# A graph network's hops on one core: twelve load slots for the weight columns in the room of the residual features, and gathered rows split in tiles of four

## The chip, the cores and the metric

The kernel runs on one core of a Trainium2 chip. The metric is the device time of one execution in microseconds, as the median of several runs; less is better. All inputs start in the core's DRAM and the output ends there.

## The reference, cut to what matters

The program is a stack of four residual graph blocks over 6250 nodes with 128 features each, and 106,250 directed edges (17 edges end in each node on average). Every block is followed by a layer norm over `x + block(x)`. The first three blocks are usual graph convolutions. The last one, which takes most of the time, has three layers, and each layer sends its features three times over the weighted edges. These nine sendings are the *hops*:

```
w = dinv[src] * edge_attr * dinv[dst]
h = node
for l in range(NUM_LAYERS):                       # 3
    out = h @ W[l, 0]
    x = h
    for k in range(1, K + 1):                     # K = 3
        x = jax.ops.segment_sum(w[:, None] * x[src], dst, num_segments=N)
        out = out + x @ W[l, k]
    y = h + out + bias[l]
    h = relu(layernorm(y) * gamma[l] + beta[l])
...
x = _layernorm(x + h)          # the x that came into this block: the residual
```

The weights of the edges are the same in all nine hops. The residual `x` is made before the first hop and read only after the last.

## The kernel before, in words

**Windows and chunks.** The nodes lie in 49 windows of 128. Destination windows are put together into 13 chunks of four windows, some of three, so that one chunk has up to 512 destination columns. A chunk fills one bank of PSUM (128 features x 512 nodes).

**A hop has two parts.** The first nine chunks (33 windows; six chunks are 512 columns wide, three are 384) are *dense*. Their edge weights have been scattered into a full matrix in DRAM, `weights`. For one chunk, TensorE multiplies the features of source window 0, 1, ... 48 (`tables[h]`) with the 128 x 512 block of that matrix which belongs to the window and the chunk, and sums all 49 products in one bank, `acc` (L1086). The matrix is too large for SBUF, so it is streamed from DRAM in every hop: SP issues one load for every two windows (`STEP = 2`, 512 KB or 384 KB, L453 in `columns`, called at L1084). The loads go round through six slots of the tile `weighed` (`LOADS = 6`, L913). This makes 225 loads and 441 window products in a hop; each window product shows as two instructions in the trace, hence 7938 of them.

The other 16 windows are *gathered*. Each has 19 gathers (`KG`); one gather fetches 128 rows of 128 features by index from the hop's table in DRAM (`stored`), 304 in a hop. POOL issues them one after another (L1018) into a ring of 32 row slots, `rows` (`SLOTS`). ACT then scales a fetched tile by the edges' weights into the left half of a tile `both`, rounded to TensorE's format (L1050); VectorE puts what the rounding lost into the right half (L1051). TensorE adds up both halves at once by multiplying them with a matrix of ones and zeros, `oh`, that says which row goes to which node (L1054). VectorE makes `oh` for five gathers at a time (L1034). There are 14 tiles `both` (L1049), one for each gather under way.

**What sets the order.** TensorE's order is written out by hand. The class `Stream` is a planner: it keeps a clock of its own, adds planned costs to it (a window product 0.86 us, a gathered product 0.12, a gather on POOL 1.26, a landing 7.0), and puts a gathered product between the window products at the time at which it plans its row to have landed. The block at the end runs under `tc.manual_schedule`, so that TensorE follows this order strictly: when one instruction waits, all behind it wait. `AHEAD` (L983) is 28, four less than the row slots: so many gathers may be asked for ahead of those taken. The other engines execute their instructions in their own program order as well, and wait on semaphores that the engines post to each other. SP's queue holds almost only the column loads in this stage; a load waits until TensorE has finished with the slot that it overwrites. ACT's scaling waits for the row to have landed and for TensorE to have finished with the `both` that it overwrites.

**The ends of chunks.** When a chunk's sum is ready, `hop_end` multiplies it with small matrices, updates `hid` (the layer's sum), and stores the next hop's features in DRAM (`store`, L891, from ACT's queue). The next hop's first gather needs all windows of the hop to have been stored, so each hop has a stretch at its start without gathers. In the last hop (`h == 8`) VectorE adds the residual, `xr` (L963), a last norm follows, and ACT's queue stores the result.

**The residual.** `xr` is a table in SBUF of 49 x 128 numbers for each of 128 partitions. The stage before the hops (L895 to L906, "g2") makes it chunk by chunk: `norm(xr[:, ws], r)` writes it (L899), and the first hop's features and `hid` are worked out from it. It then stays in SBUF through all nine hops.

Of the kernel before, what the change touches and what calls it, by code (L numbers as in the profile page):

```python
# [33 lines left out]
F32 = mybir.dt.float32  # L34
# [13 lines left out]
P = 128  # L48
N = 6250
E = 106250  # L50
D = 128
# [30 lines left out]
RPP = -(-(ROWS + P + KX * P // KD + 1) // P)  # L82
L = RPP * KD

SLOTS, LOADS, STEP, HOTS = 32, 6, 2, 5
GROUPS = -(-KG // HOTS)
F_KEY, F_DST = 0, KD + 2 * J
F_CELL, F_LOW, F_W = F_DST + KD, F_DST + 2 * KD, F_DST + 3 * KD
# [272 lines left out]
def usual_way(ctx, tc, a, out, dram, ident, part, first, recs, edges, counts, weights, fills, empty):  # L361
# [31 lines left out]
    def table(name, room, dt=F32):  # L393
        return tabs.tile([P, NW, D], dt, name=name, tag=f"room{room}")
# [19 lines left out]
    def turned(x, d=D):  # L414

        n = x.shape[1]
        pt = bank()
        for j in range(n):
            nc.tensor.transpose(pt[:d, j * P:(j + 1) * P], x[:, j, :], ident[:])  # L419
        t = work.tile([P, CW], F32, name="xT", tag="xT")  # L420
        nc.scalar.copy(t[:d, :n * P], pt[:d, :n * P])
        return t[:d]

    def times(n, xt, w, d=D):
        pm = bank()
        for j in range(n):
            nc.tensor.matmul(pm[:, j * d:(j + 1) * d], xt[:, j * P:(j + 1) * P], w, start=True, stop=True)  # L427
        return pm[:, :n * d].rearrange("p (n d) -> p n d", d=d)
# [398 lines left out]
    with tc.tile_pool(name="counted2", bufs=2) as counted:  # L827
        t2 = table("t2", 0, FR)
        slots = columns_room("room1")
        for c in range(NC):  # L830
            n, ws = of(c)
            nc.scalar.dma_start(xr[:, ws], bases[c][:])
            half = fetched_sums(early_parts[c] if c < AHEAD else halves[c])
            acc = counted_sum(counted, c, both(t1hi, t1lo), turns, slots=slots,
                              since=KNOWN if c < AHEAD else START[c])
            y = mean_conv(c, acc, wt["w2l"][:], half)
            nc.vector.tensor_add(y[:], y[:], xr[:, ws])
            norm(xr[:, ws], y)
            pm = times(n, turned(xr[:, ws]), wt["wconv"][:], DH)
            u = new("u", n, DH)  # L840
            nc.vector.tensor_tensor(u[:], pm, per_node(dinv, ws, DH), op=ALU.mult)
            split(t2[:, ws, :DH], t2[:, ws, DH:], u[:])


        def sym_conv(c, sums, bias, d=D):
            n, ws = of(c)
            r = new("y", n, d)
            nc.vector.tensor_tensor(r[:], sums, per_node(dinv, ws, d), op=ALU.mult)
            nc.vector.tensor_add(r[:], r[:], per_feature(bias, n))
            return r  # L850


        def next_parts(c, hi, lo, x):
            n, ws = of(c)
            u = new("u", n)
            nc.vector.tensor_tensor(u[:], x, per_node(dinv, ws, D), op=ALU.mult)
            split(hi[:, ws], lo[:, ws], u[:])

        def summed(c, parts, w):
            return times(SHAPE[c], evicted(counted_sum(counted, c, parts, turns, own=True), width(c)), w)  # L860

        t3 = table("t30", 2, FR), table("t31", 3, FR)
        for c in range(NC):
            n, ws = of(c)
            agg = evicted(counted_sum(counted, c, lambda s: [t2[:, s, :]], turns, own=True,
                                      slots=slots), width(c))
            pr = bank()
            for j in range(n):
                nc.tensor.matmul(pr[:, j * DH:(j + 1) * DH], agg[:, j * P:(j + 1) * P], stacked[:],
                                 start=True, stop=True)  # L870
            r = sym_conv(c, pr[:, :n * DH].rearrange("p (n d) -> p n d", d=DH), wt["bconv"], DH)
            nc.vector.tensor_scalar_max(r[:], r[:], 0.0)
            po = times(n, turned(r, DH), wt["wlin"][:])
            y = new("h", n)
            nc.vector.tensor_tensor(y[:], po, per_feature(wt["blin"], n), op=ALU.add)
            nc.vector.tensor_add(y[:], y[:], xr[:, ws])
            norm(xr[:, ws], y)
            next_parts(c, *t3, xr[:, ws])

        t4 = table("t40", 0, FR), table("t41", 1, FR)  # L880
        for c in range(NC):
            n, ws = of(c)
            r = sym_conv(c, summed(c, both(*t3), wt["g1"][:]), wt["gb1"])
            nc.vector.tensor_scalar_max(r[:], r[:], 0.0)
            next_parts(c, *t4, r[:])


        hop_out, hid = table("hop", 2), table("hid", 3)
        stored = [dram.tile([P * NW, D], F32, name=f"stored{i}") for i in range(2)]

        def store(ws, i, t):  # L891
            nc.scalar.dma_start(stored[i].rearrange("(p w) d -> p w d", p=P)[:, ws, :], t[:, ws])

        paced.rest()
        for c in range(NC):  # L895
            n, ws = of(c)
            r = sym_conv(c, summed(c, both(*t4), wt["g2"][:]), wt["gb2"])
            nc.vector.tensor_add(r[:], r[:], xr[:, ws])
            norm(xr[:, ws], r)  # L899
            po = times(n, turned(xr[:, ws]), wt["wk"][:, 0])  # L900
            nc.vector.tensor_tensor(hid[:, ws], xr[:, ws], per_feature(wt["bias0"], n), op=ALU.add)
            nc.vector.tensor_add(hid[:, ws], hid[:, ws], po)
            last = nc.vector.tensor_tensor(hop_out[:, ws], xr[:, ws], per_node(dinvw, ws, D), op=ALU.mult)
            store(ws, 0, hop_out)
            for i in range(2 * c, min(2 * c + 2, NG)):
                gathered_edges(i, last.ins)  # L906
# [3 lines left out]
    ohs = ctx.enter_context(tc.tile_pool(name="ohs", bufs=3))  # L910
    ps_g = ctx.enter_context(tc.tile_pool(name="ps_g", bufs=2, space=PSUM))
    fetched_rows = ohs.tile([P, SLOTS, D], F32, name="rows", bufs=1)
    weighed = tabs.tile([P, LOADS, STEP * CW], F32, name="weighed", tag="room1")  # L913

    def hop_end(h, ws, acc, t, now, gathered):

# [43 lines left out]
        nc.vector.tensor_tensor(x[:], x[:], per_feature(wt[f"beta{l}"], n), op=ALU.add)  # L960
        nc.vector.tensor_scalar_max(x[:], x[:], 0.0)
        if h == 8:
            nc.vector.tensor_add(x[:], x[:], xr[:, ws])  # L963
            o = new("u", n)
            norm(o, x)
            for j, w in enumerate(range(ws.start, ws.stop)):
                rows = P if w < NW - 1 else LAST
                nc.scalar.dma_start(out[w * P:w * P + rows, :], o[:rows, j, :])
            return
# [11 lines left out]
    class Stream:  # L981
# [56 lines left out]
        def take(self):  # L1038

            i, k = divmod(self.taken, KG)  # L1040
            if k == 0 and i % 2 == 0:
                self.acc = ps_g.tile([P, CW], F32, name="gacc")
            if k % HOTS == 0:
                g = (self.h * NG + i) * GROUPS + k // HOTS
                self.oh = self.oh_next if g else self.hot(0)
                self.oh_next = self.hot(g + 1) if g + 1 < 9 * NG * GROUPS else None
            x = fetched_rows[:, self.slot(self.taken), :]
            w = gwgt[:, i, k:k + 1]
            both = ohs.tile([P, 2 * D], FR, name="both", bufs=14)  # L1049
            nc.scalar.activation(both[:, :D], x, AF.Copy, scale=w)  # L1050
            nc.vector.scalar_tensor_tensor(both[:, D:], x, w, both[:, :D].bitcast(F32),  # L1051
                                           op0=ALU.mult, op1=ALU.subtract)
            j = i % 2
            nc.tensor.matmul(self.acc[:, j * 2 * D:(j + 1) * 2 * D], self.oh[:, k % HOTS, :], both[:],  # L1054
                             start=k == 0, stop=k == KG - 1)
            self.lands.pop(0)
            self.taken += 1
            self.clock += self.GATHERED
            if k == KG - 1 and GW[i] == PAIRS[i // 2].stop - 1:
                self.ends.append(hop_end(self.h, PAIRS[i // 2], self.acc, tables[self.h + 1], self, True))  # L1060
            if self.taken == NG * KG:
                self.h, self.asked, self.taken = self.h + 1, 0, 0
# [15 lines left out]
        def hop(self, h):  # L1078
            for c in range(ND):
                cw, acc, t = width(c), accumulator(), None  # L1080
                for s in range(NW):
                    self.wait(lambda: (h - 1, s) in self.when)
                    if s % STEP == 0:
                        t = columns(weighed[:, self.loads % LOADS, :], c, weights, F32, STEP, s)  # L1084
                        self.loads += 1
                    nc.tensor.matmul(acc[:, :cw], tables[h][:, s, :], t[:, s % STEP * cw:(s % STEP + 1) * cw],  # L1086
                                     start=s == 0, stop=s == NW - 1)
                    self.clock += self.DENSE * cw / CW
                    self.turn()
                self.ends.append(hop_end(h, of(c)[1], acc, tables[h + 1], self, False))  # L1090
# [368 lines left out]
```

## Time and profile before

| | us |
|---|---|
| median of three runs (7903.20 to 7933.64) | 7911.05 |
| the profiled execution, its own time | 7874.4 |
| its span, first to last instruction | 7872.4 |
| PE, TensorE's matmuls, busy | 5765.3 |
| POOL, the gathers' issue, busy | 4229.2 |
| VectorE busy | 3038.9 |
| ACT busy | 2116.4 |

The profile is of a single execution, which was 0.5% shorter than the median of the timed runs. It names each group of instructions by its line in the kernel, its engine and its operands: `acc<-weighed,hop` is the window product that reads `weighed` and `hop` and writes `acc`. A row of a group ends with the time for which the engine stood idle just before such instructions, and with what it waited for most. "DMA weighed<-weights" there is a column load that had not landed; "PE gacc" is a gathered product that had not been done. "SPq" is SP's queue of DMA issues. "issue" stands for time in which an engine waited for nothing that the profile shows, and "remote" or "another core or an unknown queue" for a release that the profile can't place. This program runs on one core.

Over the whole span the granted clock of TensorE is 0.854 of full speed on average; when TensorE is idle, its clock falls. The nine hops take the last 60% of the span, from 3169 us on.

### The profile page before, as it was taken

Reading aid. Unit: us, or ns where it says so; the run is one execution under the profiler, and the core shown is the slowest. Engines: PE = TensorE matmul, PEld = TensorE weight load, DVE = VectorE, ACT = ScalarE, POOL = GpSimd, SP = SyncE. Lnnn points to the kernel's source line nnn. Section 1 sums busy time; section 2 is a strip of 40 time slices with the busy share of each in tenths; the row PEclk is TensorE's granted clock in tenths of the full one; section 3 lists DMA queues with packets and bytes.
Section 4 is the critical chain, followed back from the end, with each engine's and each line's share of the span. In section 5 each row is a group of like instructions: output and inputs, shape, how many; then the busy total and the mean of one; then the engine's idle time right before and its main releaser. Section 6 shows DMA issues by size and latency. Waiting matters only on the chain. (4 is left out here: it accounts for less than half of the span.)

```text
span 7872.4 us, 74936 instructions
## 1 busy us (share of the span) xinstructions
PE 5765.3 (73%) x20184; PEld 3463.3 (44%) x20184; DVE 3038.9 (39%) x8549; ACT 2116.4 (27%) x4437; POOL 4229.2 (54%) x4207
## 2 busy tenths in 40 slices
PE   1354544339667799788787887987878879878788
PEld 0123333117555688345344453453444534434444
DVE  5344423112555356233332542333335423333355
ACT  1122212115344354222221221222212212222122
POOL 5665455640557411564664655646646456466464
PEclk8676666569878899899898998998989989989899
DMA  7453543013343344577676776776767767777776
GB/s 229 125 163 116 166 134 98 13 30 101 103 115 99 88 139 135 203 264 259 229 261 231 260 241 228 276 249 233 268 235 259 240 225 274 246 248 262 240 275 229
DMA packets 715822, 1532.71 MB, mean 195 GB/s; under 512 B 135525, under 2 KB 346873, under 8 KB 715129
## 3 DMA queue, kind: packets, MB, share of 16 engines
q1 hardware_dynamic: 536448, 1292.14, 49.1%
q0 software_dynamic: 134496, 181.90, 7.9%
q10 hardware_dynamic: 44440, 53.77, 2.0%
q8 instruction: 161, 2.64, 0.1%
q14 instruction: 277, 2.26, 0.1%
HBM read 1334.25 MB, written 193.11 MB: 194 GB/s over the span
## 5 line engine op out<-in xcount | busy, mean ns | idle before, releaser
L1086 PE MATMUL acc<-weighed,hop 128*128 128x512 f32 (+1 forms) x7938 | 3687.9, 584 | 561.7 <-DMA weighed<-weights 532.6
L1018 POOL DMA_INDIRECT rows<-stored,gsrc x2736 | 2709.3, 990 | 2055.4 <-DMA weighed<-weights 715.4
L1086 PEld LDWEIGHTS acc<-weighed,hop 128*128 128x128 f32 x7938 | 1364.6, 198 | 1664.5 <-issue 787.9
L1050 ACT ACTIVATE both<-rows,gwgt 128x128 fp32r<-128x128 f32 x2736 | 1008.5, 397 | 3093.1 <-PE gacc L1054 1400.8
L1054 PE MATMUL gacc<-both,oh 128*128 128x256 f32 x2736 | 1777.1, 657 | 13.3 <-issue 11.8
L1051 DVE SCALAR_TENSOR_TENSOR both<-rows,gwgt,both 128x128 fp32r<-128x128 f32 x2736 | 901.6, 349 | 2112.1 <-issue 1189.1
L492 PE MATMUL acc<-wides,t 128*128 128x512 f32 (+1 forms) x3105 | 948.1, 415 | 444.4 <-issue 221.7
L571 POOL DMA_INDIRECT counts<-cval,celli x833 | 857.3, 1029 | 584.4 <-issue 248.5
L571 POOL DMA_INDIRECT weights<-wval,celli x578 | 609.9, 1055 | 603.2 <-PE acc L492 423.6
L492 PEld LDWEIGHTS acc<-wides,t 128*128 128x128 f32 x3105 | 606.5, 204 | 622.7 <-issue 271.8
L1054 PEld LDWEIGHTS gacc<-both,oh 128*128 128x128 f32 x2736 | 543.5, 199 | 630.9 <-issue 496.7
L481 ACT CAST wides<-slots 128x1024 fp32r<-128x1024 uint8 (+3 forms) x687 | 569.4, 863 | 837.8 <-remote 464.8
L492 PE MATMUL acc<-widev,t 128*128 128x512 f32 (+1 forms) x2034 | 589.6, 400 | 100.4 <-DVE widev L481 61.9
L1034 DVE TENSOR_TENSOR oh<-iota,gdst 128x640 fp32r<-128x640 f16 x576 | 454.5, 789 | 510.6 <-PE gacc L1054 310.0
L695 DVE TENSOR_SCALAR oh<-iota,dloc 128x384 bf16<-128x384 f16 x833 | 228.1, 325 | 900.5 <-remote 462.3
L492 PEld LDWEIGHTS acc<-widev,t 128*128 128x128 f32 x2034 | 387.7, 198 | 178.1 <-DVE widev L481 77.3
L696 PE MATMUL pd<-oh,lw 128*4 128x384 bf16 x833 | 216.0, 382 | 272.3 <-issue 141.5
L481 ACT CAST wides<-cols 128x1024 fp32r<-128x1024 uint8 (+1 forms) x364 | 286.2, 797 | 383.3 <-PE acc L492 166.0
L481 DVE CAST widev<-cols 128x1024 fp32r<-128x1024 uint8 (+1 forms) x364 | 242.9, 671 | 299.3 <-PE acc L492 190.7
L696 PEld LDWEIGHTS <-lw 128*4 128x4 bf16 x833 | 68.7, 91 | 364.3 <-issue 323.3
L481 DVE CAST widev<-slots 128x1024 fp32r<-128x1024 uint8 (+2 forms) x237 | 154.7, 667 | 116.1 <-PE acc L492 37.9
L492 PE MATMUL half<-wides,t 128*128 128x512 f32 (+1 forms) x594 | 188.0, 397 | 0.0
(232 smaller groups left out, 2805.9 us busy)
## 6 DMA issues: line engine op xcount, KB each, us to landing
weighed<-weights SPq DMA_DIRECT2D x1296, 512.0 KB
weighed<-weights SPq DMA_DIRECT2D x648, 384.0 KB
slots<-counts SPq DMA_DIRECT2D x173, 448.0 KB
weights<-zeros SPq DMA_DIRECT2D x6, 12544.0 KB
cols<-counts SPq DMA_DIRECT2D x140, 448.0 KB
rows<-stored,gsrc POOLq DMA_INDIRECT x2736
counts<-zeros SPq DMA_DIRECT2D x10, 3136.0 KB
weights<-zeros SPq DMA_DIRECT2D x3, 9408.0 KB
```

The source lines that it names most:

```text
L481: copy(wide[:, :n * cw], t[:, r * cw:(r + n) * cw])
L492: product = nc.tensor.matmul(into[:, :cw], lhs, cols, start=s == begin and i == 0, stop=s == end - 1 and i == len(lhss) - 1).ins
L571: ins = nc.gpsimd.indirect_dma_start(out=mat[:], out_offset=bass.IndirectOffsetOnAxis(ap=celli[:, i, k:k + 1], axis=0), in_=vals[:, i, k:k ...
L695: nc.vector.tensor_scalar(oh[:], iota[:], dloc[:, k:k + 1], None, op0=ALU.is_equal)
L696: nc.tensor.matmul(acc[:], lw[:, k, :], oh[:], start=k == 0, stop=k == KD - 1)
L1018: nc.gpsimd.indirect_dma_start(out=fetched_rows[:, self.slot(self.asked), :], out_offset=None, in_=stored[self.h % 2][:], in_offset=bass.I ...
L1034: nc.vector.tensor_tensor(oh[:, :m, :], iota[:, :P].unsqueeze(1).to_broadcast([P, m, P]), gdst[:, i, ks].unsqueeze(2).to_broadcast([P, m, ...
L1050: nc.scalar.activation(both[:, :D], x, AF.Copy, scale=w)
L1051: nc.vector.scalar_tensor_tensor(both[:, D:], x, w, both[:, :D].bitcast(F32), op0=ALU.mult, op1=ALU.subtract)
L1054: nc.tensor.matmul(self.acc[:, j * 2 * D:(j + 1) * 2 * D], self.oh[:, k % HOTS, :], both[:], start=k == 0, stop=k == KG - 1)
L1086: nc.tensor.matmul(acc[:, :cw], tables[h][:, s, :], t[:, s % STEP * cw:(s % STEP + 1) * cw], start=s == 0, stop=s == NW - 1)
```

## The change

The change has three parts.

1. **Twelve load slots.** `weighed` becomes a list of two tiles of six slots each. The first lies in the room of the tag `room1`, as before; the second in the room of the tag `xr`, where the residual was. Loads take the two tiles in turn: load 0 goes to slot 0 of the first, load 1 to slot 0 of the second, load 2 to slot 1 of the first, and so on.
2. **The residual in DRAM.** A new tile in DRAM, `residual`, takes each chunk of `xr` as soon as its norm has written it. In the last hop a load from it goes into `y`, a work tile that `hop_end` has at hand, and VectorE adds `y` in place of `xr`. Both transfers are issued from ACT's queue.
3. **Tiles of four.** The halves of gathered rows, `both`, are no longer 14 tiles of one gather each, but four tiles of four gathers each (`GROUP = 4`), 16 gathers in all. A scaling and a gathered product work on one quarter of a tile. To make room, the row slots go from 32 to 30, and with them `AHEAD` from 28 to 26.

```diff
-SLOTS, LOADS, STEP, HOTS = 32, 6, 2, 5
+SLOTS, LOADS, STEP, HOTS, GROUP = 30, 12, 2, 5, 4
...
         hop_out, hid = table("hop", 2), table("hid", 3)
+        residual = dram.tile([P, NW, D], F32, name="residual")
...
             norm(xr[:, ws], r)
+            nc.scalar.dma_start(residual[:, ws, :], xr[:, ws])
...
-    weighed = tabs.tile([P, LOADS, STEP * CW], F32, name="weighed", tag="room1")
+    weighed = [tabs.tile([P, LOADS // 2, STEP * CW], F32, name="weighed", tag=tag) for tag in ("room1", "xr")]
...
         if h == 8:
-            nc.vector.tensor_add(x[:], x[:], xr[:, ws])
+            nc.scalar.dma_start(y[:], residual[:, ws, :])
+            nc.vector.tensor_add(x[:], x[:], y[:])
...
-            both = ohs.tile([P, 2 * D], FR, name="both", bufs=14)
+            if self.taken % GROUP == 0:
+                self.both = ohs.tile([P, GROUP, 2 * D], FR, name="both", bufs=4)
+            both = self.both[:, self.taken % GROUP, :]
...
-            nc.tensor.matmul(self.acc[:, j * 2 * D:(j + 1) * 2 * D], self.oh[:, k % HOTS, :], both[:],
+            nc.tensor.matmul(self.acc[:, j * 2 * D:(j + 1) * 2 * D], self.oh[:, k % HOTS, :], both,
...
-                        t = columns(weighed[:, self.loads % LOADS, :], c, weights, F32, STEP, s)
+                        t = columns(weighed[self.loads % 2][:, self.loads // 2 % (LOADS // 2), :], c, weights, F32, STEP, s)
```

## The prediction

> **What bounds the kernel now.** I read the groups of the page first, to find the line that holds the time; then the table of waits; then a table by stage, to find where in a hop the waits lie; last the chain of waits inside the worst stage. In the groups, the columns are busy time, mean ns of one | idle time before it and what ended most of it.
>
> ```profile
> L1086 PE MATMUL acc<-weighed,hop 128*128 128x512 f32 (+1 forms) x7938 | 3687.9, 584 | 561.7 <-DMA weighed<-weights 532.6
> L1018 POOL DMA_INDIRECT rows<-stored,gsrc x2736 | 2709.3, 990 | 2055.4 <-DMA weighed<-weights 715.4
> L1050 ACT ACTIVATE both<-rows,gwgt 128x128 fp32r<-128x128 f32 x2736 | 1008.5, 397 | 3093.1 <-PE gacc L1054 1400.8
> ```
>
> The nine hops run from 3169 to 7861 us, 4692 us in all, with PE busy for 3923 of them: 765 us are open to a gain. Of these 533 are waits for a column load, `weighed`. ACT's idle time counts only where PE then lacks a `both`.
>
> The stages of hop 3, in order: 80 us from its first gather, the rest of its gathers, the stretch without gathers; then 20 us inside the first (columns: length, busy us and count of PE, PEld, DVE, ACT, POOL; granted clock; DMA share; GB/s).
>
> ```profile
> 4770.60:4850.60 80.00, 42.71 (x87) 18.94 (x87) 12.44 (x34) 11.54 (x32) 54.35 (x58) 0.70 0.44 143
> 4850.60:5219.00 368.40, 328.50 (x988) 173.35 (x987) 137.32 (x356) 95.14 (x265) 243.68 (x247) 0.94 0.76 268
> 5219.00:5279.90 60.90, 60.89 (x220) 37.37 (x219) 22.48 (x55) 13.25 (x35) 1.26 (x2) 1.00 0.88 288
> 4820.00:4840.00 20.00, 4.28 (x6) 1.73 (x6) 1.31 (x3) 0.80 (x2) 9.79 (x12) 0.59 0.28 88
> ```
>
> PE is full at full clock without gathers. It idles 37 us in the first 80 us after the gathers start, and 40 in the 368 that follow. While PE lacks loads, the DMA is 28% busy: bandwidth isn't short. The chain of waits there shows what is:
>
> ```profile
> 4795.62 12.22 issue
> 4807.84 0.32 SPq L453
> 4808.16 0.05 issue
> 4808.21 0.02 SPq L453
> 4808.22 16.40 another core or an unknown queue
> 4824.62 0.02 issue
> 4824.64 0.32 SPq L453
> ...
> 4837.62 4.58 another core or an unknown queue
> 4842.21 3.12 DMA weighed<-weights
> ```
>
> A load takes 3 us, but SP issues one per 12 to 17 us. The matmul that freed the slot of the load at 4807.84 had ended at 4787.22, that of 4824.64 at 4789.16, that of 4837.24 at 4791.00: 21, 35 and 46 us earlier. At other times SP follows such an end by 0.03 us. ACT's scalings (L1050) come late in the same way. So PE's signals arrive late: from 4795 to 4838 about one in 4.3 us. From 4842.2 the whole backlog comes through within 2 us, some 10 us after POOL has stopped issuing gathers back to back because its row slots are full. Later in the hop the same returns, weaker: lags up to 11 us, about every 20 us, so some 18 times in 369 us. I don't know why PE's signals and POOL's gathers collide; the coincidence is all that the trace has.
>
> Split over all nine hops, waits for `weighed` are 340 us (40 waits) in the first 80 us after the first gather and 189 us (93 waits, mostly 2 to 4 us) in the rest; ends of chunks (transposes and small products) have 174 us in the rest.
>
> **What the Trainium skill says.** "Perfetto Trace Analysis", section "DMA Instruction — HWDGE (DVE, Sync)": the reported start of such an issue is the moment when all its semaphores are satisfied. That is why I read SP's start times as arrivals of PE's signal; the lag of 0.03 us in quiet stretches agrees. "DMA: Bandwidth & Descriptors", section "Anatomy of one DMA — SWDGE (gpsimd) path": some 2.0 us plus bytes over 436 GB/s, an estimate of 3.2 us for 512 KB (its fit is for another issue path); the trace has 3.1. "TensorE: Matmul & The Clock Gate", Part 1: an idle array falls to half clock and needs some 3.4 us of work to recover; the trace agrees, 1.04 us for a dense matmul instruction after a stall against 0.51. The same page, "The cost: per-tile semaphore tail": increments serialize at some 26 ns each. The flush agrees with that order, but 4.3 us per signal does not, and the measurement decides.
>
> **The change, part by part** (lines are those of the kernel before).
>
> *Twelve loads ahead (L1084).* Before, PE can run 6 loads or 12 windows past the last signal, afterwards 24. A window costs PE 0.87 us, with its share of gathered matmuls 1.3 at most. In a burst PE finished about 19 windows in the 60 us from the first gather to the flush. Six more loads would give 12 more windows, but PE's order is fixed, and each missing `both` halts it: 16 instead of 14 of these cover some 7 to 8 windows more. At 0.87 us this is 6 to 7 us per hop; I take off 1 for a longer burst and land at 6, bounds 4 and 11: **-54 us** (-36 to -99). In the rest the cover of the lag grows from about 12 windows x 0.95 us less 3 us of landing = 8.4 us to about 20, against lags up to 11. That covers the 189 us of waits by itself; but the scalings wait for the same signals with nearly their old depth, and ends of chunks still read their own. What is late next is thus `both`, then `pp`. I take 45% as gained: **-85 us** (0 to -150).
>
> *Clock.* After a stall of over about 3 us PE works some 4 us at half speed and loses 2. If 10 of the 133 waits go for good: **-20** (0 to -50).
>
> *Groups of four (L1049).* Matmuls at L1054 that post a signal fall, in the built program, from 2675 to 1702, those of L1086 from 3119 to 2800: -22% in all. ACT's separate waits at the scaling fall from 2696 to 674. No work is added. A row's slot comes free only with the fourth matmul of its group: 12 are always free behind the group in work instead of 13. Cost between +150 (a rival below) and a gain, if signals are what is short; I take **0**.
>
> *30 row slots.* AHEAD falls from 28 to 26 gathers, 32 us at POOL's pace of 1.25: rows land in 3 to 8 us, so the cover holds. Two gathers fewer end the burst up to 2.5 us sooner; counted in the 6 above.
>
> *Residual out to DRAM (after L899).* 13 stores on ACT's queue, at the 0.32 us that an SP issue takes: 4 us of issue, hidden by the stage's matmuls; uncovered +4. The next norm's square root is queued behind each. **+2**.
>
> *Second tile in the residual's room (L913).* Odd loads go there and must wait for the last chunk's readers and its store. In the built program SP issues loads 0, 2, 4 to 12 first, then 1. Before, load 0 was issued at 3169.1 and nine windows were done by 3182; after, PE does two, then the last chunk's transposes and products, then waits for load 1: last reader 3178.9, store landed about 3181, load 3 us. Once: **+9** (0 to +15).
>
> *Residual back (L963).* 17 loads in the last hop, issued ahead of the norm, whose result is needed 3.2 us later (7861.88 to 7865.07 in the tail). Hidden but for the last: **+2** (0 to +6), with ACT's next scalings queued behind 0.3 us.
>
> The sum: -54 - 85 - 20 + 0 + 2 + 9 + 2 = -146. On the profiled execution of 7874 us this is 7728; the median of the runs, 7911, stands 0.46% above it, so 7764, rounded to **7760**.
>
> **Rivals.** *No gain: signals are the bound, not loads.* ACT's 1400.8 us of waiting on gathered matmuls speaks for it: where signals come one per 4.3 us, `both` runs out at nearly the same moment, and each stall only changes its name. Then only the 2 more `both` count: 2 rows or 1.7 us in the burst, x 9 = -15, +13 of fixed costs: about 7909, with some of the rest perhaps 7880. Against it: in the rest 93 stalls end on `weighed`, while the gathered matmuls (L1054) have only 13 us of idle time before them in the whole program.
>
> *Slower: the groups hold `both` back.* With late signals ACT waits for a fourth matmul's post, up to three posts of 2.3 us (the rate in weak phases) later than for the first. PE's written order then halts at a gathered matmul though twelve loads lie ready. It decides from about 0.9 us per phase, where 18 x 9 x 0.9 = 146 us cancel the gain; with the gain lost and 0.5 us added to each, 7911 + 13 + 81 = 8005. Against it: fewer posts, and four slots come free at once.
>
> *Much faster: fewer signals.* If the slow delivery is a matter of their number, 22% fewer, and PE running through, shorten each phase: half of the 340 us and all of the 189, -360 + 13, from 7911: about 7565.
>
> **How the numbers follow.** The forecast has 0.58; no gain 0.16; slower 0.13; much faster 0.13. About 0.5%, 40 us, is what a measurement of this kernel can tell from no change. The forecast's own parts run from -36 + 0 + 0 + 19 to -99 - 150 - 50 + 5, that is 7894 to 7617; half of the no-gain case lies inside. To leave out no more than 2 in 10 I reach down to 7600 and up to 7910. Faster by over 0.5%: 0.58 + 0.13, plus little from the no-gain case, less 0.02 for the forecast's end near 7894: 0.71. Within: 0.15. Slower: 0.14.
>
> **What would show it.** Right: `weighed` waits in the hops fall from 533 us to under 350; loads issued late, but PE past 24 windows in a burst; stalls after it ended by `both` or `pp`; the first 80 us of a hop holding 47 to 50 us of PE instead of 43; the clock in the rest above 0.95; hop 0 some 9 us later in getting under way. Wrong: PE's idle time per hop unchanged with gathered matmuls named instead of `weighed`; the gap between an end on PE and the issue that waits for it longer than 46 us; POOL waiting longer between its gathers.

## The result and the profile after

| | before | after |
|---|---|---|
| median, us (20 runs each) | 7927.97 (7899.34 to 7977.06) | 7887.02 (7841.97 to 7939.97) |
| ratio, 95% interval | | 0.9943 (0.9922 to 0.9965) |
| profiled execution: own time, span | 7874.4, 7872.4 | 7895.7, 7893.8 |
| the nine hops in the profiled execution | 4688 | 4655 |
| idle time of PE in the first 80 us after a hop's first gather, nine hops | 357 | 279 |
| idle time in the rest of the gather phase | 394 | 413 |
| idle time in the stretch without gathers | 15 | 19 |
| length of that stretch, nine hops | 634 | 584 |

The change is a gain of 0.6%, some 41 us in the medians, where 146 had been forecast. The waits for column loads are gone nearly altogether: 533 us became 7. Only some 40 us of these came out as time. The groups of the page, with the columns as in the prediction:

```profile
L1091 PE MATMUL acc<-weighed,hop 128*128 128x512 f32 (+1 forms) x7938 | 3681.6, 581 | 336.0 <-issue 326.9
L1059 PE MATMUL gacc<-both,oh 128*128 128x256 f32 x2736 | 1733.2, 641 | 99.7 <-issue 98.0
L1055 ACT ACTIVATE both<-rows,gwgt 128x128 fp32r<-128x128 f32 x2736 | 879.2, 390 | 2895.0 <-issue 1115.7
```

PE's idle time ahead of its window products is now put down almost wholly to "issue", 327 of 336 us: no load, no `both` and no other engine ended it. The table of PE's waits from the first hop on shows how such idle time looks (total us, times, longest us), and that the ends of chunks (`pp`) now wait more often for ACT and VectorE:

```profile
PE acc L1091 <- issue: 326.9, 253, 3.1
PE gacc L1059 <- issue: 98.0, 75, 2.5
PE pp L419 <- DVE h L926: 92.6, 19, 11.8
PE pp L427 <- ACT xT L421: 69.4, 14, 11.9
```

253 waits of 1.3 us each are not the picture of an engine that lacks data, which had been 138 waits of 3.9 us. The stages of hop 3 after the change, cut as in the prediction, and 20 us inside the first:

```profile
4803.00:4883.00 80.00, 48.16 (x102) 21.53 (x101) 13.67 (x37) 12.16 (x34) 54.11 (x57) 0.68 0.45 150
4883.00:5251.00 368.00, 325.00 (x985) 172.88 (x984) 132.22 (x358) 84.28 (x266) 240.47 (x247) 0.93 0.75 263
5251.00:5310.40 59.40, 59.40 (x215) 36.55 (x214) 19.88 (x49) 10.11 (x30) 1.06 (x2) 1.00 0.94 325
4840.00:4860.00 20.00, 5.80 (x7) 2.01 (x7) 0.00 (x0) 0.00 (x0) 15.12 (x17) 0.50 0.33 102
```

The first 80 us hold 48 us of PE's work in place of 43. The 368 us that follow are as long as before, and PE idles for 43 of them in place of 40. In the 20 us of the last line PE executed 7 matmuls. PE's own timeline there (start, us, instruction [idle before and what ended it]) names no load:

```profile
4829.69 0.59 PE L1091 MATMUL acc<-weighed,hop 128*128 128x512 f32 x1
4831.82 0.59 PE L1091 MATMUL acc<-weighed,hop 128*128 128x512 f32 x1 [1.54 <-issue]
...
4836.03 1.01 PE L1091 MATMUL acc<-weighed,hop 128*128 128x512 f32 x1 [2.52 <-issue]
4838.82 1.01 PE L1091 MATMUL acc<-weighed,hop 128*128 128x512 f32 x1 [1.79 <-issue]
4841.63 1.01 PE L1091 MATMUL acc<-weighed,hop 128*128 128x512 f32 x1 [1.79 <-issue]
4845.12 1.01 PE L1091 MATMUL acc<-weighed,hop 128*128 128x512 f32 x1 [2.48 <-issue]
```

Matmuls of window products, which otherwise start every 0.43 us, start some 2.8 us apart, one at a time, and with its weight load each is two instructions: one per 1.4 us. All these starts lie a multiple of about 0.70 us apart.

By the *completion* of a matmul I mean here the moment at which an engine that waits for it goes on. The end that the trace gives for a matmul is modelled and can lie long before that moment. I counted, for each load or scaling that came late, how many of PE's instructions (matmuls and weight loads) had started between the end of the matmul it waited for and the moment at which it went. After the change these are 58, 58, 60 and 58 at 4840.23, 4857.04, 4860.54 and 4869.65, that is 29 or 30 matmuls with their weight loads. At each of these four moments PE too starts an instruction, after a long idle time:

```profile
4840.23 0.29 PEld L1091 LDWEIGHTS acc<-weighed,hop 128*128 128x128 f32 x1 [2.50 <-issue]
4857.03 0.29 PEld L1091 LDWEIGHTS acc<-weighed,hop 128*128 128x128 f32 x1 [2.52 <-issue]
4860.52 0.29 PEld L1091 LDWEIGHTS acc<-weighed,hop 128*128 128x128 f32 x1 [3.20 <-issue]
4869.64 0.29 PEld L1091 LDWEIGHTS acc<-weighed,hop 128*128 128x128 f32 x1 [1.11 <-issue]
```

In this profile the same count for nearly all loads of the nine hops (1999 of 2025) never passes 60. It is 57 to 60 for 78 of them, and 71 of these 78 went within 0.025 us of a start on PE, against one in ten of the others. **So PE can run only about 30 matmuls past the last one whose completion was seen, and more load slots don't change that.** Before the change the count is 51 to 59 from 4795 to 4839, and it passes 56 for only 4 loads of the nine hops. Six loads, which are 12 windows or 24 matmuls (48 instructions with the weight loads) and a few gathered products, end just short of the limit. The second six slots lie for the most part beyond it.

A second thing was not to be expected: of the chips that the kernels ran on, some show hardly any late completions. On those the kernel *before* takes 6225 us, not 7920. The runs below met two chips of this kind and four with late completions; each ratio is against the kernel before on the same chip.

### The profile page after: what moved, and what is told of

The parts are those of the page before. It is cut to its first block, busy times and chain, and to the rows that moved or that the text cites. A ratio compares the mean times of both kernels' runs of the same rounds, so it can differ in the third digit from the quotient of the medians.

```text
span 7893.8 us, 73018 instructions
## 1 busy us (share of the span) xinstructions
PE 5805.9 (74%) x20184; PEld 3479.6 (44%) x20184; DVE 2979.8 (38%) x8549; ACT 1995.5 (25%) x4437; POOL 4220.2 (53%) x4207
## 5 line engine op out<-in xcount | busy, mean ns | idle before, releaser
L1059 PE MATMUL gacc<-both,oh 128*128 128x256 f32 x2736 | 1733.2, 641 | 99.7 <-issue 98.0
L1055 ACT ACTIVATE both<-rows,gwgt 128x128 fp32r<-128x128 f32 x2736 | 879.2, 390 | 2895.0 <-issue 1115.7
L1056 DVE SCALAR_TENSOR_TENSOR both<-rows,gwgt,both 128x128 fp32r<-128x128 f32 x2736 | 831.6, 348 | 1525.2 <-ACT both L1055 718.8
L492 PE MATMUL acc<-wides,t 128*128 128x512 f32 (+1 forms) x3105 | 969.7, 422 | 559.6 <-ACT wides L481 316.3
```

The costliest lines, as they stand in the source:

```text
L492: product = nc.tensor.matmul(into[:, :cw], lhs, cols, start=s == begin and i == 0, stop=s == end - 1 and i == len(lhss) - 1).ins
```

## The experiments

### The two parts of the change, alone

Twelve slots with the residual in DRAM, and single tiles of halves as before:

```diff
-            if self.taken % GROUP == 0:
-                self.both = ohs.tile([P, GROUP, 2 * D], FR, name="both", bufs=4)
-            both = self.both[:, self.taken % GROUP, :]
+            both = ohs.tile([P, 2 * D], FR, name="both", bufs=14)
...
```

> Twelve slots and the residual in DRAM, 14 single tiles of halves, 30 row slots. Theory (while POOL issues gathers back to back, TensorE gets through one instruction per 1.4 us, and slots only let it run on until some 50 finished instructions are pending): the slots alone give the gain, PE idle in the first 80 us of a hop about 31 us as in the changed kernel (before: 40), the rest of the gather phase unchanged, time 0.4 to 0.6% below before. Rival (the tiles of four are needed, since the halves run out first): idle in the first 80 us stays near 38 to 40, time within 0.2% of before.

Tiles of four and 30 row slots, on the kernel before:

```diff
-SLOTS, LOADS, STEP, HOTS = 32, 6, 2, 5
+SLOTS, LOADS, STEP, HOTS, GROUP = 30, 6, 2, 5, 4
...
-            both = ohs.tile([P, 2 * D], FR, name="both", bufs=14)
+            if self.taken % GROUP == 0:
+                self.both = ohs.tile([P, GROUP, 2 * D], FR, name="both", bufs=4)
+            both = self.both[:, self.taken % GROUP, :]
...
```

> Tiles of four and 30 row slots, six load slots, residual in SBUF. Theory: as before, first 80 us idle 38 to 40 us per hop, waits for column loads about 500 us in the hops, time within 0.3% of before; fewer signals don't help, since every TensorE instruction pays and not every signal. Rival of the forecast (fewer signals are what helps): waits for loads fall by a fifth, 1% faster. Rival (groups hold halves back): up to 1% slower.

These met a chip on which the kernel before took 6224.51 us: 0.9992 (0.9986 to 0.9999) for the slots and 1.0012 (1.0005 to 1.0018) for the tiles of four. The expectation of 0.4 to 0.6% failed there, for a reason that it hadn't considered: there was nothing to gain. To see whether that was the chip, the whole change ran again, and then the kernel before with a profile.

> The changed kernel unaltered, beside the kernel before. The four runs so far met a kernel before of 6224 us, not 7911, and PE without the slow phases. Theory (the twelve slots are worth something only where TensorE's completions come slowly): if the kernel before takes about 6220 us here, no waits for column loads in either and a ratio within 0.2% of 1, between those of the two parts measured alone (0.9992 and 1.0012); if it takes about 7900 us, the ratio of 0.994 again with PE idle near 31 us in a hop's first 80 us. Rival (the gain is of another kind, such as the order in the stages ahead of the hops): 0.5% faster in both surroundings.

It met a chip with late completions: 7876.84 against 7932.07 us, 0.9935 (0.9904 to 0.9967), and 284 us of idle time in the first 80 us of nine hops. The rival of a gain of another kind isn't settled by this alone. Against it stand the two parts, which gave 0.9992 and 1.0012 on the other chip; the whole change never ran on a chip without late completions.

> The kernel before, profiled once more. Where TensorE's slow phases are present: hops 4690 us long as in the first profile; the stage ahead of the hops 3169 us again if the difference of 55 us to both profiles of the changed kernel (3227 and 3222) comes from the change, about 3220 if the first profile of before was a short one by chance. The order of TensorE's work is the same in both kernels until 2880 us, the loss lies at 2365 to 2690 us: so chance, about 3200 to 3225. Where they are absent: about 6224 us and nearly no waits for column loads.

It met a chip without them: 6227.01 us. Here are its window products, and the stages of hop 3, first 80 us, rest and stretch without gathers:

```profile
L1086 PE MATMUL acc<-weighed,hop 128*128 128x512 f32 (+1 forms) x7938 | 3484.1, 560 | 4.1 <-DMA weighed<-weights 4.0
```

```profile
3635.00:3715.00 80.00, 70.09 (x203) 35.53 (x202) 29.52 (x75) 24.15 (x63) 61.11 (x63) 0.94 0.83 279
3715.00:4025.00 310.00, 304.67 (x1000) 167.83 (x1000) 139.92 (x354) 101.13 (x261) 236.54 (x242) 1.00 0.93 312
4025.00:4053.00 28.00, 27.89 (x95) 16.24 (x94) 7.17 (x16) 2.83 (x7) 0.48 (x2) 1.00 0.94 309
```

It is the same kernel with the same six slots, and POOL issued 63 gathers in the first 80 us, against 58: and PE waited 4 us for loads in the whole program. Of 2005 loads none was issued more than 3.5 us after the end of the matmul that freed its slot; in the first profile of before 471 were more than 5 us late. Six slots suffice where completions come in time.

The slots alone ran once more on this chip, and then on one with late completions, which is the comparison that counts:

> Twelve slots and the residual in DRAM, single tiles of halves, once more. With slow phases present, theory (slots let TensorE run on until some 50 finished instructions are pending): the whole gain of the changed kernel, 0.4 to 0.7% below before, idle in a hop's first 80 us about 31 us. Rival (tiles of four needed): within 0.2% of before. With slow phases absent: 0.999 as measured.

> Twelve slots, single tiles of halves, on a chip that shows the slow phases if one is met. Theory: the whole gain of the changed kernel, 0.4 to 0.7% below before, PE idle in a hop's first 80 us about 31 us. Rival (tiles of four needed): within 0.2%, 38 to 40 us. On a chip without slow phases: 0.999 again.

7866.18 against 7922.84 us: 0.9932 (0.9908 to 0.9957); on the chip without, 0.9989 (0.9981 to 0.9998). PE's largest waits in the hops, with late completions:

```profile
PE acc L1089 <- issue: 267.3, 188, 3.2
PE gacc L1057 <- issue: 92.0, 70, 2.2
PE pp L419 <- issue: 85.1, 15, 11.1
```

> Tiles of four, six load slots, residual in SBUF, on a chip with slow phases if one is met. The slots alone gave 0.9932 there, the whole change 0.9935 and 0.9943. Theory (the tiles of four are worth nothing): 0.997 to 1.003, waits for column loads near 530 us in the hops, idle in a hop's first 80 us 38 to 40 us. Rival (22% fewer signals help by themselves): 0.99 or less. Rival (groups hold halves back): 1.005 or more. On a chip without slow phases: 1.0012 again.

7932.99 against 7920.91 us: 1.0017 (0.9985 to 1.0049), with the waits for loads back:

```profile
PE acc L1088 <- DMA weighed<-weights: 559.3, 146, 14.4
```

The slots give all of the 0.6%, the tiles of four nothing that can be measured here. Fewer signals by 22% don't help, and a group doesn't hold a slot back so that it shows.

### Is it POOL's gathers that delay PE's completions?

The changed kernel without every second gather in hops 1 to 8. The row slot keeps older rows; PE's order, the loads, the scalings and the products are the same. Hop 0 keeps all gathers. The kernel lacks half of the gathered rows, so it is of use as an experiment alone.

```diff
-                nc.gpsimd.indirect_dma_start(
+                if self.h == 0 or self.asked % 2 == 0:
+                    nc.gpsimd.indirect_dma_start(
...
```

> The changed kernel without every second gather in hops 1 to 8 (the row slot keeps older rows; all else, TensorE's order too, is the same). With slow phases present, theory (POOL's gathers slow TensorE's completions): PE idle in hops 1 to 8 falls from 78 us a hop to under 35, time 4 to 6% below before. Rival (column loads, halves or ends of chunks set the idle time): PE idle stays above 65 us a hop, time at most 1.5% below. With slow phases absent: hop length unchanged within 2%.

> The changed kernel without every second gather in hops 1 to 8, on a chip that shows the slow phases if one is met (the kernel before near 7900 us). Theory (POOL's gathers slow TensorE's completions): PE idle in hops 1 to 8 under 35 us a hop in place of 78, time 4 to 6% below before. Rival (loads, halves or ends of chunks set the idle time): above 65 us a hop, at most 1.5% below. On a chip without slow phases: 3.5% below again.

On a chip without late completions it took 6008.59 us, 0.9652 of before (0.9633 to 0.9671); its hops 1 to 8 of 401 to 412 us, where before had 423 to 453, are more than 2% shorter, against the expectation. With late completions it took 7063.96 against 7922.84 us: **0.892** (0.8876 to 0.8963). The same execution holds its own control. The first 80 us and the rest of the gather phase of hop 0, with all gathers, and of hop 1, with half of them:

```profile
3230.70:3310.70 80.00, 50.89 (x105) 22.07 (x106) 14.20 (x40) 12.26 (x36) 54.43 (x58) 0.69 0.56 187
3310.70:3678.40 367.70, 321.67 (x987) 172.75 (x986) 133.72 (x358) 85.08 (x266) 243.03 (x247) 0.94 0.77 266
3744.20:3824.20 80.00, 74.40 (x212) 36.78 (x211) 29.91 (x81) 21.41 (x65) 44.71 (x46) 0.96 0.80 284
3824.20:4086.80 262.60, 262.60 (x848) 142.64 (x847) 115.06 (x305) 74.39 (x228) 103.73 (x107) 1.00 0.89 292
```

Hop 0 takes 513.5 us with 79 idle, hop 1 409.9 with 6. Loads, halves and chunk ends are the same in both. What is left of the stalls is a first series of gathers, 5.6 us. In the rest of the gather phase of hops 1 to 8 no load went more than 0.1 us after the end of the matmul that freed its slot. So the gathers are what makes PE's completions late on this chip. A gather that is left out takes away its issue on POOL and its transfers together, so which of the two does it isn't shown. The gain is larger than expected since the gather phase, 343 us from first to last gather instead of 448, gets shorter too; the 3.5% on the chip without late completions shows that not all of the 10.8% comes from completions.

### Fewer gathers in a row

The changed kernel with 16 row slots, so that POOL can be less far ahead (`AHEAD` falls with them from 26 to 12):

```diff
-SLOTS, LOADS, STEP, HOTS, GROUP = 30, 12, 2, 5, 4
+SLOTS, LOADS, STEP, HOTS, GROUP = 16, 12, 2, 5, 4
```

> The changed kernel with 16 row slots in place of 30 (12 gathers ahead of those taken). Theory: POOL can issue only some 16 gathers before it must pause, so the slow phase at a hop's start ends after 25 to 30 us in place of 63, PE idle in the first 80 us falls from 31 to about 15 us, time 1 to 2% below before. Rival (gathers need their lead, rows land late): gathered products wait for rows, gather phase longer, 1 to 3% slower than before.

> The changed kernel with 16 row slots, once more. With slow phases present, theory (gathers issued back to back cause them, and 16 slots end the series sooner): idle in a hop's first 80 us about 15 us in place of 31, time 1 to 2.5% below before. Rival (it is the number of gathers and not their bunching): each hop as long as with 30 slots, time within 0.7% of before. With slow phases absent: 1.0007 as measured.

> The changed kernel with 16 row slots, on a chip that shows the slow phases if one is met. Theory (a series of gathers back to back causes them, 16 slots end it sooner): idle in a hop's first 80 us about 15 us, time 1 to 2.5% below before. Rival (the number of gathers decides): within 0.7%. On a chip without slow phases: within 0.1% again.

Without late completions 1.0007 (0.9998 to 1.0015) and 1.0003 (0.9994 to 1.0012): 16 slots cover the landing of a row. With them 7755.58 against 7922.84 us, **0.9784** (0.9746 to 0.9822). Hop 3:

```profile
4793.50:4873.50 80.00, 65.02 (x170) 31.62 (x169) 23.28 (x64) 18.01 (x53) 53.87 (x56) 0.85 0.63 221
4873.50:5238.50 365.00, 314.76 (x978) 170.78 (x976) 128.33 (x346) 82.41 (x258) 243.38 (x248) 0.94 0.76 263
5238.50:5281.20 42.70, 42.70 (x149) 25.61 (x149) 14.10 (x35) 6.23 (x19) 1.11 (x3) 1.00 0.93 329
```

The idle time in the first 80 us of this hop falls from 32 us to 15, as expected; over the nine hops it is 172 us, 19 a hop, in place of 279. The first series of gathers, counted as long as no two start more than 1.35 us apart, is 32 long in most hops, where with 30 slots the longest are of 50: POOL goes on while slots come free. The rest of the gather phase gains nothing (453 us of idle time in nine hops, after 413 and 427 with 30 slots), and what PE got done earlier shortens the stretch without gathers, 59 us to 43.

### Gathers spaced

A first attempt put a memset on POOL beside each gather:

```diff
+    pause = ohs.tile([P, D], F32, name="pause", bufs=1)
...
-        DENSE, GATHERED, SMALL, WIDE, PACE, LAND, AHEAD = 0.86, 0.12, 0.29, 0.45, 1.26, 7.0, SLOTS - 4
+        DENSE, GATHERED, SMALL, WIDE, PACE, LAND, AHEAD = 0.86, 0.12, 0.29, 0.45, 1.42, 7.0, SLOTS - 4
...
+                nc.gpsimd.memset(pause[:], 0.0)
                 self.pool += self.PACE
```

> The changed kernel with a small memset on POOL ahead of each gather's successor, so that gathers come about every 1.4 us in place of 1.25, and the plan's PACE 1.42. Theory (gathers in immediate succession starve TensorE): the slow phases get shorter or vanish, PE idle in a hop falls from 79 us to under 50, time 2 to 4% below before. Rival (the number of gathers decides, not their spacing): idle unchanged, time within 1% of before or up to 2% slower because the gather phase is 43 us longer by plan.

It met a chip without late completions and took 6768.56 us, 1.0869 of before. The edit didn't do what was meant: POOL's timeline in hop 0 has runs of gathers and then often 15 to 20 memsets together, at times more (205 ns each), since nothing tied a memset to its gather. Hops 0 and 1 took 666 and 681 us. It tells nothing about spacing. The next edit leaves POOL alone. With only 16 slots POOL must wait for PE to take rows, and PE takes them in the planner's order; so a larger planned `PACE` (1.36, 1.50) was meant to space the gathers:

```diff
-        DENSE, GATHERED, SMALL, WIDE, PACE, LAND, AHEAD = 0.86, 0.12, 0.29, 0.45, 1.26, 7.0, SLOTS - 4
+        DENSE, GATHERED, SMALL, WIDE, PACE, LAND, AHEAD = 0.86, 0.12, 0.29, 0.45, 1.36, 7.0, SLOTS - 4
```

> The changed kernel with 16 row slots and the planner's PACE 1.36 in place of 1.26: with few slots POOL is bound to TensorE's order, so this spaces the gathers at 1.36 us. On a chip with slow phases, theory (POOL's rate decides how fast TensorE's instructions complete): idle in the rest of the gather phase falls from 50 us to about 30, hop 480 us in place of 500, time 3 to 5% below before. Rival (spacing within such a small step changes nothing, the number of gathers does): idle as with 1.26, time 2 to 2.5% below before or nearer to it. On a chip without slow phases: 0.5 to 3% slower than before, since the gathers end later.

> The same with PACE 1.50. On a chip with slow phases, theory: idle beside gathers under 20 us a hop, but some 40 us at the hop's end without dense work, hop about 480 us. Rival: hops longer than 500 us, as the end is added to unchanged slow phases. On a chip without slow phases: hop 470 us, 6% slower than before.

7617.30 and 7537.55 against 7920.91 us: **0.9598** (0.9562 to 0.9634) and **0.9511** (0.9473 to 0.9550). Hop 3 with 1.50:

```profile
4685.50:4765.50 80.00, 66.67 (x171) 32.45 (x170) 20.90 (x56) 15.02 (x43) 52.45 (x54) 0.87 0.72 246
4765.50:5144.00 378.50, 354.34 (x1126) 194.91 (x1124) 143.74 (x381) 92.81 (x282) 244.96 (x249) 0.96 0.83 289
5144.00:5153.80 9.80, 4.30 (x7) 2.03 (x7) 3.28 (x7) 1.58 (x4) 0.95 (x1) 0.50 0.17 28
```

Over nine hops the rest of the gather phase idles 453 us with 1.26 and 16 slots, 319 with 1.36 and 243 with 1.50. For 1.50 that is 27 us a hop, more than the 20 expected beside gathers; the mean hop of 477 us is as expected. And the phase is hardly longer: 80 + 365, 80 + 375 and 80 + 379 us in hop 3, for 304 gathers some 1.47 to 1.51 us each. On this chip POOL's real rate had been near 1.5 all along, while the plan said 1.26 (on a chip without late completions the kernel before had 1.30). So the gathers were not much more widely spaced: with 1.50, 76% of those in the rest still start within 1.35 us of the one before, with 1.26 80%. A plan that admits the real rate puts more window products beside the gathers: 1126 matmuls in the rest in place of 978. Late completions did get fewer: of the loads issued in the rest of hops 1 to 8, 460 of 1313 were more than 5 us late with 1.26, 377 of 1469 with 1.36 and 120 of 1534 with 1.50. Why they did, with the spacing so little changed, and how much of the gain is due to the better plan alone, the runs don't separate.

> 16 row slots and PACE 1.36 once more, to see what the version costs on a chip without slow phases. There the kernel before has 15 to 35 us of idle time in a hop to lose and a hop of 424 to 454 us, and the gathers alone now take 304 x 1.36 = 413 us plus 11 before and some 20 after them: 0.5 to 3% slower than before. On a chip with slow phases 0.960 again.

> The same with PACE 1.50. On a chip without slow phases: 304 x 1.50 = 456 us of gathers, hops near 475 us, 5 to 8% slower than before. On a chip with slow phases 0.951 again.

These met another chip with late completions, so what these versions cost without late completions stays open. The ratios held, 0.9585 (0.9563 to 0.9606) and 0.9478 (0.9442 to 0.9515), with 8050.76 us before.

### The stage ahead of the hops

The profiled execution of the changed kernel started its first window product at 3227 us, that before at 3173. Was that a loss that hid a larger gain?

> The kernel before, one more profile, for the stage ahead of the hops on a chip with slow phases: 3169 us in the first profile, 3222 to 3252 in four profiles of changed kernels. If these 55 to 80 us are chance or the chip's, before too shows 3200 to 3260 here; if they are the change's, 3169 again.

The kernel before, profiled again on a chip with late completions, started its first window product at 3229 us. The first profile of before was a short execution by chance: at 7874.4 us it is shorter than all of its 20 timed runs. The hops took 4688 and 4713 us in the two profiles of before and 4655 and 4664 in two of after: 41 us less on the mean, the same as the difference of the medians. The change lost nothing ahead of the hops that shows.

This stage also holds a good part of the difference between the chips. Where completions come in time, the kernel before starts its first window product at 2310 us, 863 to 919 us sooner, while its hops (3903 us) are 785 to 810 us shorter. POOL fetches by index in this stage too; it wasn't taken apart.

## Why the prediction was wrong, point by point

**The step that failed** is the first sentence of "Twelve loads ahead": that PE can run 6 loads or 12 windows past the last signal before the change, and 24 after it. 24 windows are 48 matmuls. The trace after shows a limit of its own on PE, about 30 matmuls past the last completion (58 to 60 instructions with the weight loads at all four late moments of hop 3, never over 60 in the nine hops), with PE then going on at one instruction per 1.4 us, as completions come through. The prediction had seen that signals came late, and took them for messages that lag behind an engine that is free to go on. PE isn't free: in 71 of 78 cases in which a load went while PE stood at or near the limit, PE started an instruction within 0.025 us of it. What inside PE sets the limit, the trace doesn't show.

**Term by term**, in the nine hops:

- *First 80 us*, -54 us: idle time fell from 359 (mean of two profiles) to 281 us (two profiles), -77, inside its bounds of -36 to -99. What bounded it was the limit above, not the missing `both`: of the 279 us in the first profile, 273 are put down to "issue", 5 to a load and none to a `both`. That the size fits is luck.
- *Rest of the gather phase*, -85 us: idle time rose from 395 to 420 us, +24. The cover of 20 us against lags of 11 was worth nothing. The waits for loads turned into waits without a cause and into later ends of chunks: 189 us on `weighed` and 174 on `pp` became 0 and 254, with 155 us of "issue". This is the largest miss. The rival "no gain" had the better mechanism here: signals are the bound, and each stall only changed its name. But it, too, let PE run on until `both` is missing, and the new name is "issue".
- *Clock*, -20 us: PE's busy time in the hops didn't fall: 3922 and 3930 us before, 3939 and 3928 after, +7 on the mean. The granted clock in hop 3's rest went from 0.94 to 0.93; on the chip where both ran again it was 0.852 to 0.857 over whole executions before and 0.848 to 0.850 after. PE that gets one instruction per 1.4 us through is as cold as PE that waits (0.50 in the 20 us above, 0.59 in those of before).
- *Groups of four*, 0: right, 1.0017 (0.9985 to 1.0049).
- *Start of hop 0*, +9: The 21st matmul of window products came 23.1 us after the first in place of 11.8, the 31st 27.5 in place of 20.1: +7 to +11. Right. By the 100th the new kernel was ahead (97 against 109 us).
- *Stores and loads of the residual*, +2 and +2: 13 stores of 0.33 us of issue, with no loss to be seen ahead of the hops; in the last hop three additions waited 7.6 us in all for `y`, 5.6 of it once. Of that order, and in the noise.
- *Much faster by fewer signals*: refuted by the tiles of four alone. It fits that the 1.4 us are per instruction, whether it signals or not.

On the mean of two profiles each, the hops changed by -77 + 24 + 7 us, +6 of idle time ahead of hop 0's first gather and -1 in the stretches without gathers: -41, which is what the medians show.

**Signs that misled.** Several of the signs of being right came true though the mechanism was wrong: waits for `weighed` fell below 350 us, the first 80 us of hop 3 held 48 us of PE's work, and hop 0 started some 9 us later. Those that bear on the mechanism did not: PE didn't get past 24 windows, and the clock in the rest stayed below 0.95.

**Readings that don't hold.** The idle time of 765 us is 769 by the two figures beside it. The dense matmul of 0.51 us is a mean of two widths; with 512 columns one took 1.06 us cold and 0.59 warm. Lags in hop 3's rest reach 13 us, not 11. None of these changes the argument. The skill's figure for the semaphore tail of TensorE ("TensorE: Matmul & The Clock Gate", section "The cost: per-tile semaphore tail", some 26 ns for an increment) isn't reached even in the flush after a series of gathers, which the prediction took to agree with it: between 4842.21 and 4844.59 us, 45 instructions came through, 14 of them with an increment, which is 170 ns for an increment. For the 1.4 us per instruction ahead of it the measurement stands alone.

**What stays open.** Why completions are late on some chips and not on others isn't shown; each chip was met on one occasion only, so chip and occasion aren't told apart. Every execution here was recorded, on both kinds of chip, so the recording alone doesn't make completions late; but that it holds PE up together with the gathers is a rival that these runs can't exclude. What version is best without late completions wasn't measured beyond 16 slots, which cost nothing there.

## What to carry to other kernels

A wait that ends on a buffer says which buffer came last, not what is short; before adding slots, look at when the transfers were issued, and if the issue is late, at what the issuer waited for and how far the engine that it waits for may itself run ahead. More depth only pays up to the next limit behind it. When an engine's idle time turns from a few long waits with a named cause into many short ones without, as here from 138 waits of 3.9 us to 253 of 1.3, look for such a limit. Here the cure was upstream: to let the disturbing queue run less far ahead (16 row slots, -2.2%), and with that to plan with its real rate (PACE 1.50, -4.9% for both together). Both figures are from chips with late completions.

## What the runs showed of the hardware

- The same program took 6225 us on two chips and 7880 to 8057 us on four others. In the hops, some 800 us of the difference, PE's completions were late on the slower chips: with POOL's gathers every 1.25 us, PE got one instruction through in 1.4 us, in steps of about 0.70 us. The stage ahead of the hops holds the rest and wasn't taken apart.
- About 30 matmuls with their weight loads (58 to 60 instructions after the change, at most 63 with a larger `PACE`) could be unfinished on PE in the sense of their completions before it stopped; after the gathers paused, the backlog was through within some 2 us.
- At half the number of gathers the effect was nearly gone: 6 us of idle time in a hop in place of 79, in the same execution.
